# Long attention in groups of three half-column passes, for all images but the last

## Chip, cores and metric

The kernel runs on one core of a Trainium2 chip. The metric is the device time of one execution in microseconds (us); lower is better. The times are medians over repeated executions, and one further execution is recorded by the profiler.

## What is computed

The input is 8 images of 64 x 64 pixels with 256 channels, in float32. Two layers follow each other.

- Layer 0 projects each pixel to q and k (the values are k too). The first 128 channels attend inside 8 strips of 8 rows, the other 128 inside 8 strips of 8 columns, with 4 heads of 32 channels each: `softmax(q k^T / sqrt(32)) k` over the 512 pixels of a strip. A depthwise 3 x 3 convolution of `hard_swish(v)` is added, `hard_swish` taken, and the result multiplied by `w_out`.
- Layer 1 projects each of the 4096 pixels to f, g and h with 32 channels (weights divided by a spectral norm), attends over all 4096 pixels, `softmax(g f^T) h`, projects back to 256 channels, scales by gamma and adds its input.

```
s = einsum('bnd,bmd->bnm', g, f);  beta = softmax(s)
v = einsum('bnm,bmd->bnd', beta, h)
out = gamma * (v @ kv + bv) + x
```

## The kernel before

Per image the work is a row of units. There are 8 units "h" (row strips), 8 units "v" (column strips) and 2 units "l" (the long attention of layer 1, 2048 queries each). The first h unit of the next image stands ahead of the two l units, so that the order is h (7 units), v (8), h (1), l (2).

**A plain step.** A long unit has 32 steps, one for each chunk of 128 keys. In a step TensorE computes the scores of the chunk, `s` (line 1064): four products with a contraction of 32, one for each of four query blocks of 512, side by side in the four row strips of the array. They fill two of three PSUM tiles `s_0` to `s_2` of two banks each. ScalarE takes the exponentials of the two tiles (line 606, 128 x 1024 each) into `p`. One step later TensorE multiplies the weights by the values, `num_l` (line 1080): four products with 32 output channels each, side by side in the column strips. In the trace each of these float32 products has two records, so that four of them read x8.

**A group.** The v units already work otherwise: step 0 is plain, and the other three chunks are done in two groups (`PASSES`), each of three passes over half of the query columns (256 of 512) of one chunk. A group fills all three PSUM tiles: `first`, `last` and `mid`. Its scores are lines 825, its exponentials lines 838 (`first`), 839 (`last`) and 843 (`mid`), its weighted values line 871. The next group's first pass writes the tiles that held the old `first` and `last`, its second pass the one that held the old `mid`. The third pass writes a bank that the first has written in another strip, so it waits for the first; the wait is handed over by a `nop` on GpSimd's queue (line 832).

**The denominators.** VectorE adds up the weights of query blocks 0 to 2 of a long unit (`acc_l`, line 1095, 128 x 1536). Block 3 is added up by a DMA from GpSimd's queue that accumulates (`gather`, lines 1104 and 1106), the even chunks into a row of `acc_l` and the odd ones into `row_l`. In the v units VectorE does all of it, with a second addition for `mid` (`add_mid`, line 902, 128 x 1024). At the end of a unit, `sums` (line 1117) brings the denominators together on TensorE, `norm` divides, and `result` (lines 1136 and 326, `s<-act`) computes the output blocks in the same PSUM tiles as the scores; ScalarE moves them to `ot_l` (line 1146).

**What fills in.** Between the steps stand pieces of other work on TensorE, each four products of 256 columns: the projections `pq` of the next image (line 326), `pf` and `phd` (lines 987 and 1014) and the sums. Every four pieces end in evictions on ScalarE: `qh` or `kh`; `qv` (two); or `kn` and `kv`, which are followed by a `clip` into `hv`. The convolution is one pass on ScalarE (line 752) and eight on VectorE (line 756), with the halo rows of `hv` copied on GpSimd.

**The order.** All engines' orders are fixed when the program is built, by a planner (`Flow`) in the kernel's source. It keeps a clock for each engine, runs each step's scores, the values of the step before, and then such waiting tasks as fit. The table `DUE` holds the time at which each kind of task falls due. The weights `p` live in 8 slots, of which a plain step takes 2 and a group 3; the planner requires the readers of a slot to be ordered before its next writer.

```
self.half_end = max(c["act"], c["pe"] - more + PE_LAG, self.weights_free) + EXP
...
for task in self.waiting("rows"):
    if task.begin() <= self.clock["pe"] + 0.5:
        self.run(task)
```

Of the kernel before, what the change touches and what calls it, by code (L numbers as in the profile page):

```python
# [30 lines left out]
def quad(r):  # L31
    return slice(r * D, (r + 1) * D)
# [7 lines left out]

def side(h):
    return slice(h * TB // 2, (h + 1) * TB // 2)
# [7 lines left out]
    ahead1=104, ahead2=7, ahead3=1, ahead4=17, k0=-13, k1=52, k2=-18, k3=0, k4=-3, k5=18, k6=-3, k7=7,  # L50
    q0=70, q1=31, q2=-14, q3=-2, q4=70, q5=4, q6=0, q7=99, join_h0=38, join_h1=17, join_h2=23,
    join_h3=23, join_h4=-12, join_h5=26, join_h6=-17, join_h7=58, join_v0=26, join_v1=19, join_v2=20,
    join_v3=-25, join_v4=-148, join_v5=-22, join_v6=22, join_v7=-5, swish1=98, swish2=-48, swish3=-133,
    swish4=17, far_swish0=101, far_swish1=5, far_swish2=-23, far_swish3=28, far_swish4=46,
    far_swish5=-127, far_swish6=3, far_swish7=-2, result0=121, result1=-27, release_v=-9, norm_v=11,
    sums_v=-54, context_v=-34, clip_v=70, other=-91, first_ready=42, first_near=-1, first_k=1,
    first_q=-2, first_swish_v=-3, first_swish_h=54, first_conv_h=6, first_conv_v=22, near_k=-4,
    near_q=91, near_values=-10, clip=141, swish=12, conv_h0=168, conv_h1=16, conv_h2=24, conv_h3=39,
    conv_v0=17, conv_v1=23, conv_v2=29, conv_v3=69, tap=-21, join_h=-73, join_hl=24, join_v=1,
    context=-43, norm=18, release=-7, sums=66, add=26, adds_h=1, adds_v=0, group_h=0, group_v=1,  # L60
    add2=-44, add3=93, apart=6, fg0=-7, fg2=31, fg3=120, h0=32, h1=12, values_v=-74, near0=-55,
    spread0=4, spread1=72, spread_mid=61, conv_first=309, far_swish=-2,
# [35 lines left out]
class Flow:  # L98
# [5 lines left out]
    def __init__(self):  # L104
        self.t = 0
        self.clock = dict(pe=0.0, act=0.0, dve=0.0, sp=0.0)
        self.lanes = dict(pe=[], turn=[], act=[], dve=[], sp=[], pool=[], rows=[], res=[])
        self.open = None
        self.held, self.held_more, self.values_due = None, 0.0, False
        self.bank_free = 0.0  # L110
        self.half_end = self.exp_end = 0.0
        self.weights_free = self.mid_free = 0.0
        self.third = False
        self.apart = 0
        self.dve_last = None

# [134 lines left out]
    def step(self, scores, values, passes=2, third=False):  # L251
# [17 lines left out]
        if scores:  # L269
            rest = scores()  # L270
            c["pe"] = max(c["pe"], self.banks()) + DRAIN + SCORES + more
# [58 lines left out]
def tile_attention_blocks(  # L330
# [43 lines left out]
    three_e = const.tile([P, 1], F32, name="three_e")  # L374

# [144 lines left out]
    def attention(images, load_x, out_rows, exact):  # L520
# [66 lines left out]
        def place_of(n, r, h, tiles):  # L587

            first, mid, last = tiles
            if r < 2:
                return mid[:, r, side(0)] if n == 2 else first[:, r, side(h)]
            return mid[:, r - 2, side(1)] if n == 0 else last[:, r - 2, side(h)]

# [51 lines left out]
        def image(b):  # L648
# [138 lines left out]
            def window_unit(kind, i):  # L787
# [28 lines left out]
                def scores(c):  # L816
# [3 lines left out]
                    if c in passes:  # L820
                        first, mid, last = sc = [pairs.popleft() for _ in range(3)]
                        pairs.extend((first, last, mid))
                        for n, (t, h) in enumerate(passes[c]):
                            for r in range(NQ):
                                mm = nc.tensor.matmul(  # L825
                                    place_of(n, r, h, sc), lhsT=k[quad(r), t * P : (t + 1) * P],
                                    rhs=q[quad(r), side(h)], start=True, stop=True,
                                )


                                if n == 0 and r == 3:
                                    relay = nc.gpsimd.nop()
                                    handed(relay, mm)
                                if n == 2 and r == 0:
                                    handed(mm, relay)
                        at, mid_at = next(slots)
                        pt = weights_at(at)
                        nc.scalar.activation(pt[:, :2, :], first, AF.Exp, scale=D**-0.5)  # L838
                        nc.scalar.activation(pt[:, 2:, :], last, AF.Exp, scale=D**-0.5)

                        def rest():
                            pm = weights_at(mid_at, 1)
                            nc.scalar.activation(pm, mid, AF.Exp, scale=D**-0.5)  # L843
                            u[c], u["mid", c] = pt, pm

                        return rest
# [16 lines left out]
                def weighted(c):  # L863
                    if c == 0:
                        u["num"] = ps_av.tile([P, TB], F32, tag="num", name=f"num_{nm}")
                    if c in passes:
                        pt = u[c]
                        for n in (0, 2, 1):
                            t, h = passes[c][n]
                            for r in range(NQ):  # L870
                                nc.tensor.matmul(  # L871
                                    u["num"][quad(r), side(h)], lhsT=vs[kind, i][:, r, t, :],
                                    rhs=place_of(n, r, h, (pt[:, :2], u["mid", c], pt[:, 2:])),
                                    start=False, stop=(c == 2 and n == 1),
                                )
                        return
# [20 lines left out]
                def add_mid(c):  # L897

                    h = passes[c][0][1]
                    acc = u["acc"].rearrange("p (j i) c -> p i j c", j=2)[:, :, :, side(h)]  # L900
                    mid = u["mid", c].rearrange("p i (j c) -> p i j c", j=2)
                    nc.vector.tensor_add(acc, acc, mid)
# [132 lines left out]
            def global_unit(z):  # L1035
# [23 lines left out]
                def scores(c):  # L1059
                    if exact and c == 0:  # L1060
                        maxima()
                    sc = sc_tiles()
# [11 lines left out]
                    u[c] = weights_of(sc, 1.0)  # L1074

                def weighted(c):
                    if c == 0:
                        u["num"] = ps_av.tile([P, TB], F32, tag="num", name=f"num_{nm}")
                    for r in range(NQ):
                        nc.tensor.matmul(  # L1080
                            u["num"][quad(r), :], lhsT=h_sb[:, c, :], rhs=u[c][:, r, :],
                            start=(c == 0), stop=(c == 4 * NB - 1),
                        )

                rows = NQ if exact else NQ - 1

# [5 lines left out]
                def add(c):  # L1092

                    acc = acc_tile()[:, :rows, :]
                    nc.vector.tensor_add(acc, u[0][:, :rows, :] if c == 1 else acc, u[c][:, :rows, :])  # L1095

                def gather(c):

                    if c < 2:
                        u["row", c] = (  # L1100
                            rowp.tile([P, TB], F32, tag="row", name=f"row_{nm}")
                            if c else acc_tile()[:, rows, :]
                        )
                        nc.gpsimd.dma_start(out=u["row", c], in_=u[c][:, rows, :])  # L1104
                    else:
                        nc.gpsimd.dma_start(out=u["row", c % 2], in_=u[c][:, rows, :], accum_op=ALU.add)  # L1106
# [5 lines left out]
                def sums():  # L1112
                    u["sum"] = mm_tile(f"sum_{nm}")
                    for r in range(NQ):
                        parts = [u["acc"][:, r, :]] if r < rows else [u["row", 0], u["row", 1]]
# [47 lines left out]
                def last_ends(m, js):  # L1163
# [18 lines left out]
                    steps=4 * NB, scores=scores, weighted=weighted, add=add, gather=gather,  # L1182
# [56 lines left out]
        last_users = dict(acc=[], sum=[])  # L1239
# [12 lines left out]
        for u in units:  # L1252
# [4 lines left out]
            if u.kind == "l":  # L1257
                chain = None
                for c in range(1, u.steps):
                    task = flow.add(  # L1260
                        "dve", [(partial(u.add, c), [("dve", ADD if exact else ADD3)])], u.t + c + DUE["add"],
# [5 lines left out]
                    readers[u.t + c].append(task)  # L1267
                    chain = task
                gathered = []
                for c in range(0 if exact else u.steps):  # L1270
                    task = flow.add(
                        "rows", [(partial(u.gather, c), [("pool", GATHER), ("dma", SUMMED)])], u.t + c,
                        [w[c], *gathered[-2:-1]], ready=u.t + c + 1,
                    )
                    if c < 2:
                        task.after += last_users["acc"][-1:]
# [3 lines left out]
                    "pe", [(u.sums, [("pe", PROD * (1 if exact else 1.5)), ("act", COPY)])], e + 1,  # L1280
# [3 lines left out]
                last_users["acc"].append(total)  # L1284
            else:
# [78 lines left out]
        for n, im in enumerate(ims):  # L1364
# [4 lines left out]
            for i in range(NB):  # L1369
# [10 lines left out]
                for m in (0, 2):  # L1380
                    near[i, m] = flow.add(
                        "pe", product_pieces(partial(im.project, i, m), 2, ("act", EVICT)),
                        (u.t + DUE["near_k" if m else "near_q"] + (0 if last else DUE["first_near"]))
# [123 lines left out]
            l[0].ahead = {0: [pf[0], pf[1], turned[0]], 16: [pf[2], turned[1]], 24: [pf[3]]}  # L1507
# [26 lines left out]
        for u in units:  # L1534
            for c in range(u.steps if u.kind else 0):
                n = u.t + c
                if u.kind in ("h", "v") and c in u.passes:
                    at, mid_at = (place_at, place_at + 2) if c == 1 else (place_at + 1, place_at)
# [4 lines left out]
                assert place_at <= SLOTS  # L1543
# [16 lines left out]
        def unit_scores(u, c):  # L1560
            if u.kind:
                flow.require(*u.ahead.get(c, ()))
# [20 lines left out]
        with tc.manual_schedule():  # L1583
            last = None
            steps = [(u, c) for u in units for c in range(u.steps)]
            passes = [3 if u.kind in ("h", "v") and c in u.passes else 2 for u, c in steps] + [2]
# [94 lines left out]
```

## Time and profile before

| | |
|---|---|
| median of 3 executions | 3267.01 us (3264.59 to 3268.1) |
| the profiled execution | 3267.18 us |
| its span in the trace | 3265.4 us |
| TensorE busy | 3218.2 us, 99% |
| VectorE busy | 2659.7 us, 81% |
| ScalarE busy | 2653.4 us, 81% |
| GpSimd busy | 516.4 us, 16% |
| l steps in the trace | 512, with 4096 records of scores |

The profile's page gives busy time by engine, the span in 40 slices, the chain of work that ended last, and the costliest groups of instructions. A busy TensorE is not one at its peak, since its records overlap; what a step takes is read from start to start, in the chain.

### The profile page before, as it was taken

The page shows a single profiled execution, that of the slowest core. Times are in us where ns is not written, and L with a number is a line of the kernel's source. Part 1 is how long each engine was busy: PE and PEld are TensorE (multiplying, and loading weights), DVE is VectorE, ACT ScalarE, POOL GpSimd, SP SyncE. Part 2 cuts the span into 40 slices and gives each one's busy share as a digit, 9 for nine tenths or more (in the row PEclk, how much of TensorE's full clock was granted, in tenths as well). Part 3 has the DMA queues.
Part 4 walks back from the last instruction along what each step waited for, and adds up shares of the span by engine and source line. Part 5 has one row for each costly group of instructions (what it writes and reads, how often), then busy time and mean ns, then how long its engine had stood idle before and what let it go on. Part 6 is the DMA issues. An engine that isn't in the chain of part 4 may idle for free.

```text
span 3265.4 us, 83524 instructions
## 1 busy us (share of the span) xinstructions
PE 3218.2 (99%) x35348; PEld 1166.6 (36%) x35348; DVE 2659.7 (81%) x2426; ACT 2653.4 (81%) x3230; POOL 516.4 (16%) x786
## 2 busy tenths in 40 slices
PE   8999999999999999999999999999999999999998
PEld 3353233532335323343333433334323343234422
DVE  6898599975999669996699966998769986689865
ACT  6788788887888878888778887788877888778875
POOL 1002220022200222002210032100321003210132
PEclk9999999999999999999999999999999999999999
DMA  2235552356423564235642366423654236532465
GB/s 81 63 94 117 131 114 83 90 118 132 105 88 94 115 139 105 79 99 116 137 103 77 104 122 132 102 75 103 128 127 103 74 105 132 118 104 63 112 125 108
DMA packets 320655, 344.41 MB, mean 105 GB/s; under 512 B 33600, under 2 KB 198352, under 8 KB 320272
## 3 DMA queue, kind: packets, MB, share of 16 engines
q0 software_dynamic: 72000, 134.40, 23.2%
q1 hardware_dynamic: 246752, 204.04, 21.0%
q8 instruction: 280, 4.59, 0.6%
q14 instruction: 103, 0.84, 0.1%
q10 hardware_dynamic: 1520, 0.54, 0.1%
HBM read 99.78 MB, written 83.89 MB: 56 GB/s over the span
## 4 chain that ended last, share of the span: by engine, by line
PE 84%; DVE 9%; ACT 3%; DMA 2%; issue 1%; SPq 0%; DVEq 0%; ACTq 0%
PE s L1064 17%; PE num_l L1080 15%; PE pq L326 12%; PE s L849 8%; PE s L326 7%; PE num_h L878 6%; PE s L825 4%; PE num_v L871 4%; PE sum_v L917 3%; DVE act L756 3%; PE sum_h L917 3%; PE pf L987 1%; DVE acc_v L887 1%; PE num_v L878 1%; ACT p L606 1%
## 5 line engine op out<-in xcount | busy, mean ns | idle before, releaser
L606 ACT ACTIVATE p<-s 128x1024 f32<-128x1024 f32 x1664 | 1612.8, 1024 | 232.9 <-PE s L1064 143.8
L1095 DVE TENSOR_TENSOR acc_l<-acc_l,p 128x1536 f32<-128x1536 f32 x480 | 842.8, 1756 | 361.6 <-ACT p L606 357.4
L756 DVE SCALAR_TENSOR_TENSOR act<-hv,dw_sb,act 128x1024 f32<-128x1024 f32 x512 | 654.0, 1278 | 25.9 <-ACT act L752 16.5
L1064 PE MATMUL s<-gq,f 32*128 32x512 f32 x4096 | 594.1, 640 | 1.1 <-ACT ot_l L1146 1.1
L326 PE MATMUL pq<-x,wqkv_sb 128*32 128x256 f32 x8192 | 547.1, 381 | 14.0 <-DMA x<-in_xT 10.6
L1080 PE MATMUL num_l<-p,h_sb 128*32 128x512 f32 x4096 | 545.5, 605 | 0.3 <-ACT nums_l L1110 0.3
L326 PEld LDWEIGHTS pq<-x,wqkv_sb 128*32 128x32 f32 x8192 | 264.4, 110 | 431.8 <-issue 283.2
L849 PE MATMUL s<-qh,kh 32*128 32x512 f32 x2048 | 295.3, 640 | 14.0 <-ACT qh L682 13.9
L1106 POOL DMA_DIRECT2D acc_l<-p x240 | 210.3, 876 | 515.2 <-ACT p L606 477.7
L1106 POOL DMA_DIRECT2D row_l<-p x240 | 210.8, 878 | 426.9 <-ACT p L606 414.1
L878 PE MATMUL num_h<-p,vs 128*32 128x512 f32 x2048 | 272.0, 603 | 0.2 <-ACT nums_h L929 0.2
L1064 PEld LDWEIGHTS s<-gq,f 32*128 32x128 f32 x4096 | 168.7, 182 | 260.7 <-issue 247.1
L326 PE MATMUL s<-act,wout_sb 128*32 128x512 f32 x2048 | 229.2, 597 | 0.0
L1080 PEld LDWEIGHTS num_l<-p,h_sb 128*32 128x32 f32 x4096 | 80.7, 108 | 383.8 <-issue 371.3
L825 PE MATMUL s<-qv,kv 32*128 32x256 f32 x3072 | 214.3, 394 | 1.1 <-ACT p L843 0.8
L1146 ACT ACTIVATE ot_l<-s,bias_o 128x512 f32<-128x512 f32 x120 | 76.2, 684 | 161.3 <-PE s L326 154.5
L871 PE MATMUL num_v<-p,vs 128*32 128x256 f32 x3072 | 192.2, 383 | 0.0
L825 PEld LDWEIGHTS s<-qv,kv 32*128 32x128 f32 x3072 | 141.3, 183 | 80.5 <-issue 49.5
L1104 POOL DMA_DIRECT2D acc_l<-p x16 | 9.1, 566 | 1015.9 <-ACT sum_sb_h L626 508.8
L838 ACT ACTIVATE p<-s 128x1024 f32<-128x1024 f32 x128 | 131.8, 1030 | 33.5 <-PE s L825 33.4
L895 DVE TENSOR_TENSOR acc_h<-acc_h,p 128x2048 f32<-128x2048 f32 x64 | 146.1, 2282 | 7.8 <-ACT p L606 7.1
L887 DVE TENSOR_TENSOR acc_v<-p 128x2048 f32<-128x2048 f32 x64 | 146.3, 2286 | 6.4 <-PE sum_h L917 3.5
(153 smaller groups left out, 3211.5 us busy)
## 6 DMA issues: line engine op xcount, KB each, us to landing
acc_l<-p POOLq DMA_DIRECT2D x256, 256.0 KB, 3.3
row_l<-p POOLq DMA_DIRECT2D x256, 256.0 KB, 3.3
x<-in_xT SPq DMA_DIRECT2D x92, 512.0 KB, 4.0
kvia<-kt SPq DMA_DIRECT2D x128, 256.0 KB, 2.5
vs<-kvia SPq DMA_DIRECT2D x512, 64.0 KB, 2.1
out<-ot_l SPq DMA_DIRECT2D x120, 256.0 KB, 2.1
via_v<-nums_v SPq DMA_DIRECT2D x64, 256.0 KB, 2.1
shuf_v<-via_v SPq DMA_DIRECT2D x256, 64.0 KB, 2.1
```

Of the source, the lines that this page charges most:

```text
L326: nc.tensor.matmul(out[quad(r), :], lhsT=lhsT[:, quad(r)], rhs=rhs, start=start, stop=stop)
L606: nc.scalar.activation(pt[:, 2 * z : 2 * z + 2, :], sc[z], AF.Exp, scale=scale)
L756: nc.vector.scalar_tensor_tensor(o, src, wt, o, ALU.mult, ALU.add)
L825: mm = nc.tensor.matmul(place_of(n, r, h, sc), lhsT=k[quad(r), t * P : (t + 1) * P], rhs=q[quad(r), side(h)], start=True, stop=True,)
L849: nc.tensor.matmul(row_of(sc, r), lhsT=k[quad(r), c * P : (c + 1) * P], rhs=q[quad(r), :], start=True, stop=not exact,)
L871: nc.tensor.matmul(u["num"][quad(r), side(h)], lhsT=vs[kind, i][:, r, t, :], rhs=place_of(n, r, h, (pt[:, :2], u["mid", c], pt[:, 2:])), s ...
L878: nc.tensor.matmul(u["num"][quad(r), :], lhsT=vs[kind, i][:, r, c, :], rhs=u[c][:, r, :], start=(c == 0), stop=(c == 3),)
L917: nc.tensor.matmul(u["sum"][quad(r), cols], lhsT=ones[:, :D], rhs=pt, start=(n == 0), stop=(n == last),)
L1064: nc.tensor.matmul(row_of(sc, r), lhsT=f4[quad(r), c * P : (c + 1) * P], rhs=gq[quad(r), z, :], start=True, stop=not exact,)
L1080: nc.tensor.matmul(u["num"][quad(r), :], lhsT=h_sb[:, c, :], rhs=u[c][:, r, :], start=(c == 0), stop=(c == 4 * NB - 1),)
L1095: nc.vector.tensor_add(acc, u[0][:, :rows, :] if c == 1 else acc, u[c][:, :rows, :])
L1106: nc.gpsimd.dma_start(out=u["row", c % 2], in_=u[c][:, rows, :], accum_op=ALU.add)
```

## The change

- `PASSES` of the long units: all images but the last now do chunks 0 and 1 as plain steps and the other 30 in 20 groups of three passes (`GROUPS`), with the functions of the v units, made common (`group_scores`, `group_weighted`, `gain_mid`). A unit has 22 steps instead of 32.
- The denominators: chunks 0 and 1 are added for all four blocks by VectorE. Of each group VectorE adds blocks 0 to 2 of the four-block part and, in a second addition, `mid`; the gather adds block 3 of the four-block part, once a group, all into one row `row_l`.
- The planner takes the time at which the scores' inputs are ready as a bound beside the banks (`scores_ready`), and the first image's first q products have their own due time (`first_near_q`).
- `DUE` has other values throughout (`add` 26 before, -312 after, among them).
- Nine products of a constant tile by itself (`warm`) stand ahead of everything on TensorE.

The diff, cut to its core:

```diff
+GROUPS = {
+    2 + g: tuple(
+        (2 + (3 * g + k) // 2, (3 * g + k) % 2) for k in range(3)
+    )
+    for g in range((CHUNKS - 2) * 2 // 3)
+}
...
-            c["pe"] = max(c["pe"], self.banks()) + DRAIN + SCORES + more
+            c["pe"] = max(c["pe"] + DRAIN, self.banks() + DRAIN, self.scores_ready) + SCORES + more
...
+    warm = mm_tile("warm")
+    for _ in range(9):
+        nc.tensor.matmul(warm[:, :P], lhsT=ones, rhs=ones, start=True, stop=True)
...
+        def group_scores(u, c, group, lhsT, rhs, scale):
+            first, mid, last = sc = [pairs.popleft() for _ in range(3)]
+            pairs.extend((first, last, mid))
+            for n, (t, h) in enumerate(group):
+                for r in range(NQ):
+                    mm = nc.tensor.matmul(
+                        place_of(n, r, h, sc), lhsT=lhsT(r, t), rhs=rhs(r, h), start=True, stop=True,
+                    )
+                    if n == 0 and r == 3:
+                        relay = nc.gpsimd.nop()
+                        handed(relay, mm)
+                    if n == 2 and r == 0:
+                        handed(mm, relay)
...
+            nc.scalar.activation(pt[:, :2, :], first, AF.Exp, scale=scale)
+            nc.scalar.activation(pt[:, 2:, :], last, AF.Exp, scale=scale)
+            def rest():
+                pm = weights_at(mid_at, 1)
+                nc.scalar.activation(pm, mid, AF.Exp, scale=scale)
...
@@ global_unit
+                passes = {} if exact or b == images[-1] else GROUPS
+                steps = 2 + len(passes) if passes else 4 * NB
...
-                    acc = acc_tile()[:, :rows, :]
-                    nc.vector.tensor_add(acc, u[0][:, :rows, :] if c == 1 else acc, u[c][:, :rows, :])
+                    acc, n = acc_tile(), NQ if passes and c == 1 else rows
+                    nc.vector.tensor_add(
+                        acc[:, :n, :], u[0][:, :n, :] if c == 1 else acc[:, :n, :], u[c][:, :n, :]
+                    )
+                def add_mid(c):
+                    gain_mid(u["acc"], u["mid", c], passes[c][0][1])
...
+                    k = 0 if passes else c % 2
+                    if c >= (3 if passes else 2):
+                        nc.gpsimd.dma_start(out=u["row", k], in_=u[c][:, rows, :], accum_op=ALU.add)
+                        return
...
-                for c in range(0 if exact else u.steps):
+                for c in () if exact else u.passes or range(u.steps):
                     task = flow.add(
                         "rows", [(partial(u.gather, c), [("pool", GATHER), ("dma", SUMMED)])], u.t + c,
-                        [w[c], *gathered[-2:-1]], ready=u.t + c + 1,
-                    )
+                        [w[c], *(gathered[-1:] if u.passes else gathered[-2:-1])], ready=u.t + c + 1,
+                    )
```

## The prediction

> **What bounds the kernel now.** I read the page first. TensorE is busy for 99% of the span and holds 84% of the chain that ended last:
>
> ```profile
> PE 3218.2 (99%) x35348; PEld 1166.6 (36%) x35348; DVE 2659.7 (81%) x2426; ACT 2653.4 (81%) x3230; POOL 516.4 (16%) x786
> ...
> PE 84%; DVE 9%; ACT 3%; DMA 2%; issue 1%; SPq 0%; DVEq 0%; ACTq 0%
> ```
>
> Next the table by stretches, for one image's seven h units, its eight v units and its two l units (us, then busy time of PE, PEld, DVE, ACT, POOL):
>
> ```profile
> 1261.30:1371.00 109.70, 107.54 (x1138) 35.63 (x1134) 100.75 (x99) 88.04 (x114) 4.89 (x18) 1.00 0.31 92
> 1371.00:1459.30 88.30, 88.08 (x1228) 44.06 (x1224) 84.72 (x90) 76.28 (x92) 0.00 (x0) 1.00 0.32 91
> 1874.70:2065.70 191.00, 191.00 (x1918) 59.76 (x1914) 135.05 (x98) 156.47 (x188) 58.54 (x78) 1.00 0.62 125
> ```
>
> VectorE has 56 us free in the long stretch (191.0 - 135.05), but only 12.6 us in the other two together. ScalarE has 34.5 us free in the long one. So a long step lasts as long as TensorE's instructions in it. The chain, in order of time, shows them from start to start:
>
> ```profile
> 1201.92 1.07 PE s L1064 x8
> 1202.99 1.00 PE num_l L1080 x8
> 1203.99 0.43 PE pq L326 x8
> 1204.42 1.07 PE s L1064 x8
> ```
>
> A plain step without a piece takes 1.07 + 1.00 = 2.07, with one piece 2.50. A piece is eight records of 256 columns in 0.43, so eight of 512 stream in 0.86: of the 2.07, 0.35 go into the two turns between row strips and column strips. What a group takes is seen in a v unit:
>
> ```profile
> 1454.73 1.51 PE s L825 x24
> 1456.24 1.43 PE num_v L871 x24
> ```
>
> **1. Fewer turns on TensorE.** A group without a piece is 1.51 + 1.43 = 2.94 for one and a half chunks. Three chunks cost 3 x 2.07 = 6.21 before and 2 x 2.94 = 5.88 after: 0.33 less. Each changed unit has 10 such threes, and 14 units change (7 images): 140 x 0.33 = **-46 us**, if nothing else makes TensorE wait.
>
> Half-width passes need more weight loads: for three chunks 48 instead of 24 for the scores, and as many for the values. The rows have that price in them: per 256 columns the group's run is hardly longer (1.51 against 1.5 x 0.86 + 0.21 of turn = 1.50). So I take nothing more. The Trainium skill speaks against the change here: "TensorE: Matmul & The Clock Gate", section "LDWEIGHTS (loading the stationary operand)", says that a load takes its columns divided by 1.2 ns, whatever the contraction, so 107 ns for 128 columns. By that alone, with nothing overlapped, the 24 added score loads would be 2.6 us for three chunks and some 360 us in all; the v row, which has them, doesn't show it.
>
> **2. Waits for PSUM banks.** A plain step leaves one of three tiles free, a group none. How ScalarE empties them is seen after the group that starts on TensorE at 1404.45:
>
> ```profile
> 1405.69 1.02 ACT L838 ACTIVATE p<-s 128x1024 f32<-128x1024 f32 x1 [0.43 <-PE s L825]
> 1406.61 1.02 ACT L839 ACTIVATE p<-s 128x1024 f32<-128x1024 f32 x1
> 1407.52 1.03 ACT L843 ACTIVATE p<-s 128x1024 f32<-128x1024 f32 x1
> 1408.42 1.25 ACT L752 ACTIVATE act<-hv,dwb_sb,dw_sb 128x1024 f32<-128x1024 f32 x1
> ```
>
> The exponentials begin 1.24 after the group (1.18 with nothing ahead), and `mid` ends at about 4.1. The next group's second pass needs `mid`, and its first pass covers 0.43: two groups cannot follow each other in less than about 3.7. TensorE's own 2.94 + 0.43 k for k pieces reaches that only with two (3.80). The program order of the changed kernel shows the pieces: of 280 long groups 154 have two, 70 have three or more, 14 stand before an output block, 14 have one, 7 a transpose (0.58), 21 none. Per changed image that is 3 x 0.77 (none) + 2 x 0.34 (one) + 0.13 (transpose) = 3.1 us.
>
> ScalarE's other work widens some. Between `mid` and the next `first` it has about 0.8. One or two evictions of 0.59 to 0.85 from start to start fit. In the order of ScalarE, the second unit has `kn`, `kv` and the clip (0.59 + 0.57 + some 0.7 = 1.8) ahead of an empty group, and the convolution's pass (1.13 to its successor) ahead of two; following `mid`'s end from group to group, that adds 1.2. A copy of 0.53 between `last` and `mid`, at the transpose, adds 0.5. Two output runs stand ahead of a group, whose second pass needs both last evictions: 0 to 0.5 each, I take half, 0.5. Sum 3.1 + 1.2 + 0.5 + 0.5 = 5.3, with 0.1 to 0.2 of small ones 5.4 per image: **+38 us**. The ends are 22 (no such work in the way) and 47 (ScalarE's full durations instead of starts, full output waits).
>
> **3. VectorE.** A unit had 31 additions of 1.757 = 54.5 us. It gets one of 2.28 (line 887's size), 20 of 1.757 and 20 of `mid`'s size, from this row:
>
> ```profile
> L902 DVE TENSOR_TENSOR acc_v<-acc_v,p 128x1024 f32<-128x1024 f32 x64 | 78.4, 1225 | 6.2 <-ACT p L843 0.5
> ```
>
> Together 61.9: +7.4 a unit, 15 an image, 104 in all. Cover: the 56 us free in the long stretch. A group of 3.80 leaves 3.80 - 2.98 = 0.8 for other work. The order shows what that pushes out: between an image's first and last long addition stand 13 convolution taps instead of 15 (1.28 each), and one swish of 0.69 less: some 3.3 us per image go to the h and v units, which have 12.6 free. I take **0**, and keep 0 to 7 x 3.3 = 23.
>
> **4. GpSimd and the gathers.** Gathers fall from 32 to 20 a unit (each 0.88 of GpSimd); this is off the path. They now form one chain, and the relay that a group's third pass waits for sits in the same queue. The order puts the next group's relay ahead of a group's gather, so the gather starts about 0.7 after the next group's start, and the relay after it is needed 3.8 + 0.86 later. In between lie 0.88 of issue and the previous gather's landing:
>
> ```profile
> DMA to landing us min/median/max: 3.2/3.3/6.9
> ```
>
> 3.3 fits into a period of 3.7 or more; the worst, 6.9, would hold a relay by 0.1. The halo copies (1.3 to 3.3 us in the long stretch) fit likewise. SP's queue has no new transfer. I take **0**, at most 0.1 for each of a few.
>
> **5. The start.** The first two products, ahead of the first scores, run at half speed:
>
> ```profile
> 5.61 3.64 PE L326 MATMUL pq<-x,wqkv_sb 128*32 128x256 f32 x32 [5.61 <-DMA x<-in_xT]
> 10.05 3.64 PE L326 MATMUL pq<-x,wqkv_sb 128*32 128x256 f32 x32 [0.80 <-ACT kh L697]
> 14.50 1.14 PE L849 MATMUL s<-qh,kh 32*128 32x512 f32 x8 [0.81 <-ACT qh L682]
> 15.57 1.93 PE L326 MATMUL pq<-x,wqkv_sb 128*32 128x256 f32 x32
> ```
>
> The same 32 records take 1.93 later, from 15.57 on. Two products could save 2 x 1.71 = 3.4. The nine warm products need only `ones`, set at 1.1, and run while TensorE waits for x until 5.6. By the profile the gain is 0 to 3.4; I take **-2**. The same page of the Trainium skill, Part 1, says that about 3.4 us of sustained work raises the clock, in windows that don't start with the kernel: by it the whole 3.4 may come or only half. The trace agrees that short work doesn't suffice: 3.64 busy, 0.80 idle, 3.64 busy, and only then 1.93.
>
> **6. The new due times and waits.** They also reorder the h and v units. Pieces there are 46 per image instead of 48, of the same kinds. What can be won is TensorE's idle time there, 2.4 per image (109.70 - 107.54 and 88.30 - 88.08), 17 us; as much can be lost. I take 0.
>
> **The sum.** The profiled execution took 3267.2 (span 3265.4 and 1.8 around it), the median of the runs is 3267.0, so they may be used alike. 3267.2 - 46 + 38 + 0 + 0 - 2 + 0 = 3257.2.
>
> **Rivals.**
>
> (a) *Most of the 46 stays.* If the bank waits are at their low end (22), the start gives 3.4 and the h and v units half of their 17: 3267.2 - 46 + 22 - 3.4 - 8 = 3232. For it: 224 of the 280 groups have two pieces or more. Against it: two pieces leave only 0.1 of slack over 3.7.
>
> (b) *Slower: VectorE in the h and v units.* It is busy for 92% and 96% of them. The taps that leave the long stretch must be done before the joins, which feed the contexts and then `pf`; if VectorE ends last there, each moved microsecond counts: 3267.2 - 46 + 47 + 23 - 2 = 3289 with the bank waits at their high end, 3280 at 38. It decides from about half of the 23 us on: with 38, that is 3269, slower than before. For it: hardly any idle time of VectorE. Against: 12.6 us are free per image against 3.3 needed.
>
> (c) *It doesn't do what it says.* The order rules that out: 280 groups and 344 gathers instead of 512 stand in the program.
>
> **How the numbers follow.** This kernel's time can be told from no change at about 0.2%, 6.5 us, so "same" is 3260.5 to 3273.5. Forecast, 3245 to 3270: chance 0.50, of which 0.32 faster and 0.18 same. (a): 0.15, all faster. (b), to 3289 and beyond: 0.35, of which 0.05 same and 0.30 slower. Together 0.47, 0.23, 0.30. The range leaves out half of (a)'s lower part and the end of (b): 3233 to 3287. The forecast's own range is 3245 to 3270.
>
> **What would show it.** Start to start, a long group with two pieces takes 3.80, an empty one before a group 3.7 to 4.6; the long stretch of an image stays near 190 instead of falling to 184.5. VectorE busy rises to about 2764 us. The first scores start at about 12.5 instead of 14.5. It is wrong if groups with two pieces take over 3.9 (then banks, gathers or relays bind), if GpSimd's relay ends waits of TensorE, or if the h and v units change by more than 3 us an image.

## The result, and the profile after

The change makes the kernel slower: 3350.89 us (median of 4 executions, 3348.6 to 3356.34) against 3266.22 (4 executions), a ratio of 1.0261 with a 95% interval of 1.0246 to 1.0276. The forecast was 3257, with a range up to 3287. The profiled execution has a span of 3348.6.

The head of the page, and the two lines of the chain that ended last, in shares of the span by engine and by line:

```profile
PE 3240.7 (97%) x42086; PEld 1479.7 (44%) x42086; DVE 2763.4 (83%) x2566; ACT 2657.2 (79%) x3230; POOL 374.7 (11%) x618
...
PE 81%; DMA 11%; ACT 3%; issue 3%; DVE 1%; POOLq 0%; SPq 0%; POOL 0%; ACTq 0%; DVEq 0%
PE s L622 15%; DMA row_l<-p 11%; PE s L891 10%; PE pq L341 10%; PE num_l L650 7%; PE num_h L911 7%; PE s L341 7%; PE num_v L650 5%; PE sum_v L947 4%; PE sum_h L947 3%; PE s L1099 3%; PE num_l L1118 3%; PE num_v L911 2%; PE pf L1017 2%; PE s L1182 1%
```

TensorE is no longer busy for 99%, and DMA has 11% of the chain instead of 2%, all of it in one transfer: the gather, `row_l<-p`. VectorE's 2763.4 is the forecast's 2764, and it has 1% of the chain.

The table by stretches shows where the time lies. For one image the seven h units, the eight v units, and for another image its two l units (us, then busy time of PE, PEld, DVE, ACT, POOL):

```profile
1294.30:1403.50 109.20, 107.08 (x1103) 35.09 (x1099) 102.72 (x100) 84.83 (x107) 4.05 (x12) 0.98 0.30 88
1403.50:1493.40 89.90, 89.90 (x1264) 45.88 (x1260) 83.33 (x90) 77.31 (x95) 0.34 (x3) 1.00 0.33 93
1920.00:2127.10 207.10, 195.46 (x2906) 103.57 (x2902) 154.45 (x121) 160.87 (x194) 38.67 (x57) 0.99 0.40 86
```

The long stretch has grown from 191.0 to 207.1, and TensorE, which was never idle in it, now is for 11.6 us; the h stretch is no longer than before (109.7), and its 2.1 of idle time were there before too. Over the whole execution, from the first score of one stretch to that of the next: the l stretches of the seven changed images take 1344.0 before and 1430.6 after (+86.6), h +3.6, v +9.2, the single h units ahead of l -11.4; the first scores start 3.1 earlier, and the last image's l is 1.7 shorter. Together +83.2, as the spans say (3348.6 - 3265.4).

What holds the long stretch is read from the chain, in order of time, in a part of it:

```profile
1987.46 3.31 DMA row_l<-p
1990.77 0.02 issue
1990.80 0.02 POOLq L1146
1990.82 0.59 issue
1991.40 0.01 POOLq L628
1991.42 4.91 DMA row_l<-p
1996.33 0.03 issue
1996.35 0.02 POOLq L1146
1996.37 0.59 issue
1996.96 0.01 POOLq L628
1996.97 3.29 DMA row_l<-p
...
2000.91 5.28 DMA row_l<-p
2006.19 0.02 issue
2006.21 0.02 POOLq L1146
2006.23 0.59 issue
2006.82 0.03 POOLq L628
2006.84 0.04 issue
2006.89 0.71 PE s L622 x8
```

A gather lands (1990.77). GpSimd's queue, which waited for that on line 1146, starts the next gather 0.65 later (1991.42), and at the same moment the relay behind it (line 628) comes through. That gather lands after 4.91, and so on: TensorE isn't in this chain for seven gathers in a row, from 1972.71 to 2006.19 (the last four are shown). In the changed units 240 of the 266 gathers that follow another start 0.63 to 0.68 us after its landing, nearly all of them after 0.64 or 0.65; 24 of the other 26 are among the first three links of a unit. Over the 240 it is 4.40 from gather to gather on average, where a group with two pieces has 3.80 of TensorE's work. The timeline of TensorE shows the other end, the group that began at 2003.90:

```profile
2003.90 1.15 PE L622 MATMUL s<-gq,f 32*128 32x256 f32 x16
2006.89 0.71 PE L622 MATMUL s<-gq,f 32*128 32x256 f32 x8 [1.84 <-POOLq L628]
```

Its first two passes run, and the third waits 1.84 for the relay, which stood behind a waiting gather. What the gathers' line says in all (who waited for it, us and times):

```profile
  POOL row_l L1146: 192.9, 58
  PEld sum_l L1163: 48.4, 14
...
DMA to landing us min/median/max: 3.2/3.4/7.2
```

The queue waits for landings, and at the end of each of the 14 units the sums wait for the last gather, 48.4 us in all.

The arithmetic of one unit: 20 landings of 3.7 on average and 19 times 0.64 make 86. In a first l unit TensorE would issue its 20 groups in 75.7 (measured below with the chain split); here they take 77.4 to 83.2, and the last gather lands 13 after the last group started instead of 7.

### The profile page after: what moved, and what is told of

The parts are those of the page before. It is cut to its first block, busy times and chain, and to the rows that moved or that the text cites. A ratio compares the mean times of both kernels' runs of the same rounds, so it can differ in the third digit from the quotient of the medians.

```text
span 3348.6 us, 96685 instructions
## 1 busy us (share of the span) xinstructions
PE 3240.7 (97%) x42086; PEld 1479.7 (44%) x42086; DVE 2763.4 (83%) x2566; ACT 2657.2 (79%) x3230; POOL 374.7 (11%) x618
## 4 chain that ended last, share of the span: by engine, by line
PE 81%; DMA 11%; ACT 3%; issue 3%; DVE 1%; POOLq 0%; SPq 0%; POOL 0%; ACTq 0%; DVEq 0%
PE s L622 15%; DMA row_l<-p 11%; PE s L891 10%; PE pq L341 10%; PE num_l L650 7%; PE num_h L911 7%; PE s L341 7%; PE num_v L650 5%; PE sum_v L947 4%; PE sum_h L947 3%; PE s L1099 3%; PE num_l L1118 3%; PE num_v L911 2%; PE pf L1017 2%; PE s L1182 1%
## 5 line engine op out<-in xcount | busy, mean ns | idle before, releaser
L670 ACT ACTIVATE p<-s 128x1024 f32<-128x1024 f32 x824 | 799.3, 1026 | 95.2 <-PE s L891 66.9
L1135 DVE TENSOR_TENSOR acc_l<-acc_l,p 128x1536 f32<-128x1536 f32 x340 | 597.0, 1756 | 306.9 <-ACT p L635 262.2
L634 ACT ACTIVATE p<-s 128x1024 f32<-128x1024 f32 x408 | 418.8, 1027 | 150.3 <-PE s L622 149.4
L622 PE MATMUL s<-gq,f 32*128 32x256 f32 x6720 | 492.5, 403 | 44.6 <-POOLq L628 36.2
L341 PE MATMUL pq<-x,wqkv_sb 128*32 128x256 f32 x8192 | 517.2, 380 | 7.9 <-ACT qv L749 5.2
L635 ACT ACTIVATE p<-s 128x1024 f32<-128x1024 f32 x408 | 418.2, 1025 | 24.2 <-PE s L622 22.4
L650 PE MATMUL num_l<-p,h_sb 128*32 128x256 f32 x6720 | 424.3, 386 | 0.0
L639 ACT ACTIVATE p<-s 128x1024 f32<-128x1024 f32 x408 | 421.6, 1033 | 0.0
L622 PEld LDWEIGHTS s<-gq,f 32*128 32x128 f32 x6720 | 309.2, 185 | 241.8 <-issue 100.4
L1146 POOL DMA_DIRECT2D row_l<-p x296 | 259.3, 876 | 1073.5 <-PE s L622 215.5
L659 DVE TENSOR_TENSOR acc_l<-acc_l,p 128x1024 f32<-128x1024 f32 x280 | 343.4, 1226 | 27.5 <-DVE acc_l L1135 0.9
L650 PEld LDWEIGHTS num_l<-p,h_sb 128*32 128x32 f32 x6720 | 190.6, 110 | 195.9 <-issue 100.7
L650 PE MATMUL num_v<-p,vs 128*32 128x256 f32 x3072 | 192.6, 383 | 0.0
L920 DVE TENSOR_TENSOR acc_h<-p 128x2048 f32<-128x2048 f32 x64 | 146.2, 2284 | 18.1 <-PE sum_h L947 16.9
```

What stands on the lines that cost most here:

```text
L341: nc.tensor.matmul(out[quad(r), :], lhsT=lhsT[:, quad(r)], rhs=rhs, start=start, stop=stop)
L622: mm = nc.tensor.matmul(place_of(n, r, h, sc), lhsT=lhsT(r, t), rhs=rhs(r, h), start=True, stop=True,)
L634: nc.scalar.activation(pt[:, :2, :], first, AF.Exp, scale=scale)
L635: nc.scalar.activation(pt[:, 2:, :], last, AF.Exp, scale=scale)
L639: nc.scalar.activation(pm, mid, AF.Exp, scale=scale)
L650: nc.tensor.matmul(u["num"][quad(r), side(h)], lhsT=lhsT(r, t), rhs=place_of(n, r, h, (pt[:, :2], u["mid", c], pt[:, 2:])), start=False, s ...
```

## Experiments

Each is compared with the kernel before on the same chip. Theory A is the one that came out of the trace: the gathers of a unit are one chain, slower than TensorE, and relay and sums wait behind it.

**Two rows again.** The chain is split in two; nothing else of the change is touched, but for a third part in the sums and one buffer fewer of `kt`, to make room.

```diff
...
-                    k = 0 if passes else c % 2
-                    if c >= (3 if passes else 2):
+                    k = c % 2
+                    if c >= (4 if passes else 2):
...
-                        parts = [u["acc"][:, r, :]] + ([] if r < rows else [u["row", 0 if passes else 1]])
+                        parts = [u["acc"][:, r, :]] + ([] if r < rows else [u["row", 0], u["row", 1]] if passes else [u["row", 1]])
```

> The changed kernel with the gathers in two chains (even and odd groups into two rows), all orders else the same; the kt buffer is single to make room, and sums has 14 more products (12 us at most). Theory A, one gather chain binds: each gather starts 0.644 us after the one before has landed, 4.40 us from gather to gather, against 3.80 of TensorE work in a group with two pieces. With two chains a gather has 7.6 us: the third passes wait no more (71 us before), the waits of sums at the unit ends go, and the clock stays up. Long stretch 189 to 193 us per image instead of 204.5; total 3255 to 3275. Rival B, the groups' bank waits and ScalarE's other work bind and the gathers only follow: over 3330. Rival C, the relay's place in GpSimd's queue: as A, told apart by e2.

Measured: 3269.08, ratio 1.0015 (1.0005 to 1.0024). The long stretch of one image, and a part of the chain that ended last:

```profile
1473.10:1665.70 192.60, 191.39 (x2910) 103.61 (x2906) 152.11 (x119) 159.06 (x193) 38.73 (x59) 1.00 0.43 93
...
1934.69 1.57 PE s L622 x24
1936.27 1.43 PE num_l L650 x24
1937.70 0.86 PE pq L341 x16
1938.56 1.51 PE s L622 x24
```

Here the chain consists of TensorE alone (over the whole execution DMA has 1% of it), a group with two pieces takes 3.80 (median), and by the two ratios 80 of the 85 us are gone. The landings are the same (mean 3.71, against 3.68 after): the gathers aren't quicker, only no longer all in one series.

**The kernel before, with one row.** The reverse: only the chain is put into the old kernel, which has 32 gathers a unit and neither groups nor relays in its l units.

```diff
...
-                        nc.gpsimd.dma_start(out=u["row", c % 2], in_=u[c][:, rows, :], accum_op=ALU.add)
+                        nc.gpsimd.dma_start(out=u["row", 0], in_=u[c][:, rows, :], accum_op=ALU.add)
...
-                        parts = [u["acc"][:, r, :]] if r < rows else [u["row", 0], u["row", 1]]
+                        parts = [u["acc"][:, r, :]] if r < rows else [u["row", 0]]
```

> The kernel before with its gathers in one row instead of two, so in one chain; its long steps are plain and have no relay. Theory A, a chain of gathers costs landing and 0.644 us each: 64 gathers an image at 3.9 to 4.4 us are 250 to 282 us instead of a long stretch of 191, for 8 images 470 to 730 more: 3740 to 3990. Rival C, gathers only hurt through relays behind them: 3265 to 3300.

Measured: 3923.59 (2 executions), ratio 1.2013 (1.1991 to 1.2035): theory A's price, not its rival's. The chain by engine, and two links of it:

```profile
PE 47%; DMA 37%; issue 7%; DVE 5%; ACT 3%; POOL 0%; SPq 0%; POOLq 0%; ACTq 0%; DVEq 0%
...
1499.75 3.28 DMA row_l<-p
1503.02 0.02 issue
1503.05 0.02 POOLq L1103
1503.06 0.60 issue
1503.66 3.27 DMA row_l<-p
```

The same 0.64 from landing to start. The gathers follow each other every 4.24 on average (3.54 to land, the rest from landing to start), where a step took 2.98 before (191 for 64). No relay is needed here: the slots of `p` aren't freed, and the exponentials wait for the gathers, 555.5 us in all.

**No gathers.** The change without the gathers of the groups' units: block 3's share of the groups is left out of the denominators.

```diff
                 def gather(c):
...
+                    if passes:
+                        return
...
```

> The changed kernel without the gathers of the groups (block 3's share of them is left out of the denominators), all orders else the same. Theory A: 3240 to 3262, the long stretch at 187 to 190 us per image: what is left over TensorE's 184.5 is the bank waits, forecast at 5.4 per image. Rival B: over 3330.

Measured: 3231.83, ratio 0.9895 (0.9878 to 0.9911), lower than expected. The long stretch is 190.9 and the h units 104.5 instead of 109.7. Against the two-row version it also lacks two of the three parts of block 3's sums and their 0.86 each (a step with the sums takes 4.64 with three parts, 3.78 with two in the kernel before, 2.92 with one here), 24 us; the other 13 lie in the h units, and why stays open. The run bounds from below what a cured chain could give.

**Every other gather.** VectorE adds block 3 of the odd steps itself (a larger addition), so that the chain has half the links.

```diff
-                    acc, n = acc_tile(), NQ if passes and c == 1 else rows
+                    acc, n = acc_tile(), NQ if passes and c % 2 else rows
...
+                    if passes and c % 2:
+                        return
```

> The changed kernel with block 3 of every other group added by VectorE (2.28 instead of 1.757 us, 10 a unit, 74 us in all) and gathered of the others alone: one chain, with two groups of time for each gather. Theory A: 3255 to 3275, with VectorE's additions hidden in the long stretch. If VectorE is short there, up to 74 more. Rival B: over 3330.

Measured: 3270.61, ratio 1.0017 (1.0008 to 1.0027); the long stretch 193.4. One row does little harm if its links have twice the time.

**The relay in SyncE's queue.** The gathers stay one chain, but GpSimd's queue no longer holds the relay.

```diff
-                        relay = nc.gpsimd.nop()
+                        relay = nc.sync.nop()
```

> The changed kernel with the relay of a group's third pass on SyncE's queue instead of GpSimd's, where the gathers are. Rival C, the relay behind a waiting gather is all of the loss: 3255 to 3275, with the gather chain as slow as before. Theory A: the chain still needs 20 x 4.4 = 88 us a unit; the wait moves from the third pass to the weights' slots and to sums at the unit end. 3310 to 3350. Rival B: no change, 3350.

Measured: 3564.86, ratio 1.0909 (1.0891 to 1.0927): a miss for all theories. The waits of the whole execution name the reason:

```profile
PEld s L622 <- SPq L628: 222.7, 82, 9.1
PE s L622 <- SPq L628: 191.8, 72, 8.7
```

Of the 222.7, 180.0 lie in the v units, whose relays now stand behind SyncE's own transfers: a v stretch takes 115 to 123 instead of 90. Mostly these are not transfers that wait but transfers being issued, one after the other at about half a microsecond each: of the 156 us for which TensorE's products waited so in the v units, SyncE was issuing transfers in 137. The long stretches keep the change's 201 to 209. The run doesn't say how much of these the relay costs and how much the sums and the slots of `p`, since the new queue holds the relay up as well.

**VectorE adds all.** No gathers in the groups' units, and VectorE adds all four blocks (0.52 more for each addition).

```diff
-                    acc, n = acc_tile(), NQ if passes and c == 1 else rows
+                    acc, n = acc_tile(), NQ if passes else rows
...
+                    if passes:
+                        return
...
```

> The changed kernel without gathers in the groups: VectorE adds block 3 of every group too (20 a unit at 2.28 instead of 1.757 us, 148 us in all), and sums has one product less (24 us less than with two rows). All orders else the same. If the long stretch's idle time of VectorE hides it: 3232 to 3245, as without the gathers. If VectorE ends last, up to 80 more: 3300. The e5 run, with half of it, lost 1 us per image in the long stretch, so I take 3250.

Measured: 3295.03, ratio 1.0088 (1.0072 to 1.0103), a miss. VectorE has 2902 us of work (88%), and the chain by engine reads:

```profile
PE 70%; DVE 20%; issue 5%; ACT 3%; DMA 1%; SPq 0%; POOL 0%; DVEq 0%; ACTq 0%
```

VectorE's 20% here against 1% in the change: it can take the change's own 104 us more, but not another 139.

**Groups in the first unit alone,** with all of that unit's additions on VectorE, no gathers there, and the planner's costs adapted; the second unit in plain steps with its two rows.

```diff
-                passes = {} if exact or b == images[-1] else GROUPS
+                passes = {} if exact or z or b == images[-1] else GROUPS
...
```

> Groups in the first long unit of an image alone, where the program order has two pieces or more after nearly every group, added by VectorE without gathers; the second unit has plain steps with two rows as before; the planner knows of both. Bank waits theory: the first unit keeps 3.3 - 1.0 us of its gain, the second loses nothing: long stretch 187 to 189, total 3240 to 3255. If VectorE or the new order binds: 3265 or more.

Measured: 3259.88, ratio 0.9982 (0.9972 to 0.9991). The sign is as expected, the size isn't: the long stretch is 194.4, not shorter than before; the gain lies in the h units (106.1 instead of 109.7), the unit ahead of l (11.1 instead of 13.2) and the start, against losses in l and v (89.9 instead of 88.3). Seven sums have one part fewer than before (7 x 0.86 = 6.0), as much as the whole gain of 5.5 to 6. It is the one version here with all of the work that beats both kernels, by 0.18%.

**The warm products alone,** in the kernel before.

```diff
+    warm = mm_tile("warm")
+    for _ in range(9):
+        nc.tensor.matmul(warm[:, :P], lhsT=ones, rhs=ones, start=True, stop=True)
```

> The kernel before with the nine warm products alone. The first scores start 3 us sooner. If the first image keeps this: 3261. If it waits for transfers that come no sooner, and gives it back in its first units: 3264.

Measured: 3263.43, ratio 0.9993 (0.9983 to 1.0002), not told apart from no change. The first scores start at 11.3 instead of 14.5; what of that 3.2 reaches the end is at most 0.0017 x 3265 = 5.5 us and may be nothing.

**Due times and groups, one without the other.** Three runs: no groups, but the new due times (`passes = {}`); two rows with the due times of the kernel before; and two rows with groups in the first unit alone.

> The changed kernel without groups in the long units: 32 plain steps a unit and two rows for the gathers, as before, but with the new due times, the planner's new bound and the warm products. It measures the forecast's terms 5 and 6 (start, due times) together. Theory A (the whole loss of the change lies in the chain of gathers; the new due times are a small gain by themselves): the long stretch as before, 191 us an image, the h units between 104.5 and 107.5 instead of 109.7, the v units 90 instead of 88.3, the first scores at 11.4; 3230 to 3258. Rival (the due times gain only together with groups): 3262 to 3285.

> The changed kernel with two rows for the gathers, and with the due times of the kernel before (the first q products at -1 as before). Theory A: the groups are worth about nothing in the long stretch once the chain is split (192 to 194 us an image against 191), and the other stretches are as before (109.7, 88.3, 13.2): 3262 to 3288. Rival D (the new due times are what keeps the groups from gaining, by putting pieces where banks wait): the long stretch falls to 187 or less and the time to 3245 or less.

> Groups in the first long unit of each image alone, with two rows for the gathers; the second unit in plain steps as before; the rest as in the changed kernel. Theory A: without the extra additions that VectorE had in the other version of this (3259.9, with a long stretch of 194.4), the long stretch is 190 to 192.5 and the time 3238 to 3262. Rival (VectorE was not what cost there): 3256 to 3275 with a long stretch of 194 or more.

| long stretch of an image (us), time | due times before | due times after |
|---|---|---|
| no groups | 191 to 194, 3266.2 | 199.3, 3303.87, ratio 1.0118 (1.0103 to 1.0134) |
| groups in the first unit, two rows | | 195.6, 3291.09, ratio 1.0078 (1.0065 to 1.0092) |
| groups in both, two rows | 188.5 to 189.9, 3641.03, ratio 1.1154 (1.1139 to 1.1169) | 192.6, 3269.08, ratio 1.0015 (1.0005 to 1.0024) |

All three expectations missed: theory A had the due times as a small gain and the groups as worth nothing. In the right-hand column the groups shorten the long stretch, by about half for each unit (3.7 and 3.0). But neither part of the change stands alone. With the new due times and plain steps the pieces come in clumps: of the 448 steps of seven images 189 have no piece and 112 have four, where the kernel before has 15 and 28, and 259 with one. A step without a piece takes 2.07 on TensorE and two exponentials of 1.03 on ScalarE, which leaves little room for evictions. That is the likely reason why these 189 take 2.22 on average and up to 2.97 (4.0 us an image over 2.07), while the 112 take 3.88 instead of 3.79 (1.4 an image). With 5.3 more pieces an image that have moved into the stretch (2.3 us) this accounts for the 7.3 by which it is longer.

The left-hand column doesn't show that the groups shorten it. With the old due times and groups the long stretch is the shortest of all, but it has only 55 pieces of `pq`, where the kernel before has 80: the other 25 (10.8 us) stand in the h units, and with them it would be about 199. It has fewer taps (the convolution's passes on VectorE) too, 10 or 11 instead of 15 to 16 in the two-row version, while a v stretch has 25 instead of 17: the additions, due early, push them out. The h, v and l stretches of an image then are

```profile
1394.80:1534.60 139.80, 125.00 (x1355) 43.66 (x1351) 105.77 (x102) 95.86 (x126) 6.15 (x19) 0.99 0.27 80
1534.60:1637.30 102.70, 95.76 (x1164) 45.43 (x1160) 87.85 (x94) 76.52 (x92) 0.42 (x3) 0.93 0.25 74
1655.10:1843.60 188.50, 183.05 (x2662) 99.61 (x2658) 140.96 (x109) 147.15 (x172) 34.54 (x50) 1.00 0.42 90
...
ACT p L670 <- DVE acc_v L920: 113.7, 60, 4.7
```

h and v are 30 and 14 longer than before, 10.8 of the 30 for the pieces. The last line, from ScalarE's waits, names one mechanism: exponentials wait for slots of `p` that VectorE hasn't added up yet. VectorE has 22% of the chain in this run, against 9% before. How much of the 377 us is VectorE's isn't settled: the run also has one buffer of `kt` and spends 152 us at half of TensorE's clock.

## Why the prediction was wrong, point by point

**4, the gathers, is the step that failed.** It said that "3.3 fits into a period of 3.7 or more; the worst, 6.9, would hold a relay by 0.1". It takes every gather to start on its schedule, 0.7 after a group's start, and prices nothing but the landing. Three things are wrong in it, and the trace of before held the numbers for the first two.

- *The period of a chain is landing plus start.* From the landing to the next gather's start pass 0.64, in the change and in the kernel before with one row, and in before itself wherever a gather came right behind the landing of its row's last one (54 of 480). The median of 3.34 and 0.64 make 3.98 (measured median period 3.99), over the 3.80 of a group with two pieces.
- *A chain adds means, not medians.* The median landing of before is 3.3, its mean 3.64, because one in twenty takes 5 or more. So the period to be set against 3.80 was 4.28.
- *A late gather isn't made up for.* The worst case was priced as one relay held by 0.1. In a chain that is slower than its consumers each gather starts later than the one before, until the relay, and with it TensorE, goes at the chain's pace.

Right-sized from before's own landings, a unit has 20 x 3.64 + 19 x 0.64 = 85.0 of chain. Where TensorE sets the pace, a first unit has 73.8 from its first gather to its last (the two-row version) and 3.6 for the last landing, 77.4: each first unit would lose some 7.6, in its groups or at its sums. The second units, with output blocks between their groups, lose about as much: 98 to 103 from first gather to last instead of 91.6 (94.8 in one). The prediction had named the sign of it: groups with two pieces take 4.07 on average, over its 3.9.

Measured, the change against its two-row version: from the second passes' starts to the third passes' pass 193.8 us in all instead of 144.2, so 50 for the relays, and the sums wait 48.4 for the last gathers. Against these 98 the stretches show 98.7: the l stretches are 85.4 longer (1430.6 against 1351.2 less 6.0 for the third part of seven sums) and the h stretches, which hold the other seven, 13.3. TensorE's clock, which drops after such waits (last section), has a part in it that the runs don't separate. It is 23 us at most: at half clock the change spends 61 us, the two-row version 15.

**1, fewer turns: held.** Changes between row strips and column strips, counted in the trace, fall from 132 to 92 in the two long units of an image. A group's rows in the two-row version are 1.51 and 1.43, so 2.94, as forecast; the 0.165 less than a plain step and a half are the forecast's 6.6 an image, 40 x 0.165. Rival (a), by which most of it stays, isn't what happened: the waits of 2 are some 33 us in all, not 22, and the two-row version without its third parts would be 7 us shorter than before, not 35.

**2, bank waits: held in size.** They can be read in the two-row version, where the chain is gone: an image's stretch was 191.0 (images 4 to 6 before); less 6.6, plus 2.6 for the six pieces more that lie in it now and 0.86 for the third part of the sums, is 187.9; measured are 192.6. So 4.7 an image, against a forecast of 5.4. It is what is left over after 1, so other waits may be in it. Its place was only partly as forecast: of the three empty groups of an image one takes 3.67 from start to start in the two-row version, and two 2.94 to 2.98 instead of 3.7 to 4.6. The wait then shows in a later group: one with four pieces takes 6.05 behind an empty one and 4.67 in the median.

**3, VectorE: 0 held for the change.** Busy time as forecast (the free time in h and v is 12.5 by the rows, not 12.6), 1% of the chain; in the two-row version, where the gathers no longer hold it up, the chain has 10% of it, against 9% before. Rival (b) isn't what happened. Its mechanism is real, though: with the old due times VectorE has 22% of the chain, in a kernel that is 377 us slower.

**5, the start: held at the start.** The first scores come 3.1 earlier (11.41), near the high end of 0 to 3.4; whether it reaches the end isn't resolved.

```profile
1.15 4.21 PE L393 MATMUL warm<-ones 128*128 128x128 f32 x18 [1.15 <-POOL ones L386]
5.94 1.93 PE L341 MATMUL pq<-x,wqkv_sb 128*32 128x256 f32 x32 [0.58 <-DMA x<-in_xT]
```

Both products after 4.21 of warming take 1.93 instead of 3.64, so the whole doubling came.

**6, the due times: right only as a sum.** With the chain split, h changes by -3.8 over all images (with 6.0 in it for the third part of seven sums), v by +12.4, the unit ahead of l by -11.4: -9 without that part. But 30 pieces (12.9 us) have moved from these units into the long stretches; without that they would be some 4 longer, inside the 17. And the term was thought of as something that could be had or left: by itself it costs 39.6 us (the kernel without groups).

With the chain cured the kernel is at 1.0015 of the one before, 4.8 us longer, and 14 x 0.86 = 12.0 are the third part of its sums, which the change doesn't have. Less these it would be 7 shorter, where the forecast was 10 shorter. So the other terms hold together, within 3 us, and it was the chain that the forecast lacked. Without it the change would have been worth 0.2 to 0.3%, by this sum and not by a run: bank waits eat most of the turns saved.

## What to carry to other kernels

When a change merges two alternating chains of dependent transfers into one, set landing *plus* the time from a landing to the next start, taken as a mean, against the pace of the engine that feeds the chain; being off the path on average is not enough, since lateness adds up over the chain. Look at what else stands in the queue where the chain waits: a signal that another engine needs within a microsecond doesn't belong behind transfers that wait, as in GpSimd's queue here, nor behind a row of transfers being issued, as in SyncE's. And due times are tuned for one structure: judge a structure and its due times together, since either alone can cost more than both bring.

## What was not expected of the hardware

- An accumulating transfer of 256 KB started 0.64 us after the landing of the one that it waited for, in the change, where the relays stand in the same queue, and in the kernel before with one row, which has none there (0.02 and 0.02 for the wait, then 0.59 or 0.60 in which nothing is recorded).
- Short idle times of TensorE were followed by half its clock. The table by stretches around the end of an l unit, where TensorE waits 3.6 for the last gather; the third number from the end is the granted clock as a share of the full one, and after it come DMA share and GB/s:

```profile
1706.00:1713.00 7.00, 7.00 (x96) 2.69 (x88) 6.34 (x6) 7.00 (x10) 0.99 (x2) 1.00 0.65 146
1716.02:1722.85 6.83, 5.74 (x22) 1.26 (x26) 3.76 (x7) 2.36 (x3) 0.00 (x0) 0.50 0.01 1
```

After the change there are 12 such times of 3.41 or 6.83 us, and one of 6.4 that the end of the execution cuts off, 61 us in all; before there are one of 3.41 and one of 7.0 at the end. The Trainium skill, "TensorE: Matmul & The Clock Gate", Part 1, says that the clock drops after at least one idle window of some 3.4 us, and that the windows run freely. The lengths, 3.41 and 6.83, agree. The condition agrees less well: the 12 follow idle times of 1.6 to 3.6 us by TensorE's records, 10 of these under 3.4, while five idle times of 2.2 to 2.4 had no such effect. What decides between them isn't settled here.
